# A selective-scan kernel on one NeuronCore: two groups of transposes, the first sum of each output group, and eight more C tokens change their places

## The chip, the cores and the metric

The kernel runs on one core of a Trainium2 chip. The metric is device time in microseconds (us) of one launch. Before the change it is 18172.63 us, the median of 3 runs (18170.29 to 18190.06).

The engines of the core are named as the profile names them: PE (TensorE, matmuls; its weight loads are PEld), DVE (VectorE), ACT (ScalarE), POOL (GpSimd) and SP (SyncE, which issues the DMAs). Each engine runs its own queue of instructions strictly in the order in which the program issued them, and waits at an instruction whose inputs or buffers are not ready.

## What is computed

Layer 0 is a convolution block (1x1 expand, 3x3 depthwise, squeeze and excite, 1x1 project) on a 32x96x56x56 image. Layer 1, which the change touches, applies two selective-scan blocks to the image's 3136 positions as a sequence, and then a fused 1x1 convolution with batch norm. Cut to what matters:

```python
xs, z = jnp.split(layernorm(seq) @ in_w, 2, axis=-1)
xc = silu(causal_conv4(xs))
dt, Bm, Cm = split(xc @ xproj_w)                 # 6 + 16 + 16 columns
delta = softplus(dt @ dt_w + dt_b)               # 192 channels
dA  = jnp.exp(delta[..., None] * A)              # 192 channels x 16 states
dBx = delta[..., None] * Bm[:, :, None, :] * xc[..., None]
h   = scan(h[t] = dA[t] * h[t-1] + dBx[t])       # along the 3136 tokens
y   = einsum('blds,bls->bld', h, Cm) + Dp * xc
seq = seq + (y * silu(z)) @ out_w
```

## The kernel before, in words

Layer 1 works in units. A unit is one chunk of 784 tokens (a quarter of an image) in one of the two scan blocks; there are 128 chunks, so 256 units. A unit has 192 x 16 = 3072 recurrences, which are 24 scans of 128 partitions x 784 tokens (`scan`, L1052, on DVE). The program is written by hand as one loop over steps, and a step is one scan. Scan t of a unit belongs to channel group k = t // 8 (three groups of 64 channels), to state quartet j = (t % 8) // 2, and to half p = t % 2.

A scan needs two inputs. `da` = exp(A delta) is made on ACT (`decay`, L1004). The other, delta x B, comes in two ways:

- For j = 1, 2, 3 POOL multiplies u = delta x by a broadcast B for a pair of scans, four steps ahead (`inject`, L1041).
- For j = 0, that is for scans 0, 1, 8, 9, 16 and 17, PE makes it in PSUM: `fill` (L1018) multiplies a transposed piece of u, the tile `ut`, by a diagonal arrangement of B. One fill is issued in the step before its scan. Its PSUM buffer is one of two that it shares with `da`, so it waits until the scan two before its own has ended. The tiles `ut` of a unit, one for each group k, are made by `turn_u` (L848: four PE transposes into one PSUM bank of a ring of two) and copied out by `keep_u` (L854 and L855, on ACT).

What follows a scan: its pair of results is multiplied by C, the first LP tokens of each half by DVE (`product`, L1060, from a copy of C that ACT puts into PSUM, `bring`, L1029), the rest by POOL (`rest`, L1068). PE sums the product over the states into the group's tile y (`reduce`, L1099, four matmuls a pair, LAG = 4 steps after the pair's second scan). Before a group's first sum, ACT puts Dp x into that tile (`seed`, L1086); since there is one y tile, this waits until DVE has multiplied the former group's finished y by z (`gated`, L1110, LAG + 1 steps behind).

Beside the scans, the same loop prepares later units and finishes the unit before: each helper has a due time in steps in the lists of `prepare` and `finish`. Due time 48 of a unit is its own scan 0. Within a step the fraction says where it is put: under 0.05 at the step's head, before `seed` and `decay`; 0.05 to 0.08 after `fill` and before `reduce`; from 0.08 on at the step's end. Before the change the transposes of the second group are due at 53.6 (end of step 5) and their copies at 54.2, those of the third group at 54.3 (end of step 6) and 55.01 (head of step 7); fills for the scans 8 and 9 are issued in the steps 7 and 8, those for 16 and 17 in 15 and 16.

Of the kernel before, what the change touches and what calls it, by code (L numbers as in the profile page):

```python
# [24 lines left out]
NL, NS, DIN, RANK, KC = 2, 16, 192, 6, 4  # L25
LC = 784
HB = LC // 2
LP = 416
NQ = L // LC
RB = HB // W  # L30
DG = 8
# [29 lines left out]
def conv_mamba_kernel(ctx, tc, a, out):  # L61
# [43 lines left out]
    with ExitStack() as ph:  # L105
# [119 lines left out]
        for i in range(NHB):  # L225
            t = hp3.tile([128, H + 2, W + 2], F32, name=f"hpad{i}", tag=f"hpad{i}")
# [303 lines left out]
    with ExitStack() as ph:  # L530
# [14 lines left out]
        def bank(name):  # L545
            return pp.tile([128, 512], F32, name=name, tag="p")

        def wt(shape, tag, bufs, n):
            return work.tile(shape, F32, name=f"{tag}_{n}", tag=tag, bufs=bufs)
# [135 lines left out]
        def prepare(n):  # L685
# [92 lines left out]
            def keep(tag, bufs, ps, k):  # L778
                if k == 0:
                    d[tag] = wt([128, NB, HB], tag, bufs, n)  # L780
                if tag == "dl":
                    s.activation(d[tag][:, k, :], d[ps, k][:, :HB], AF.Identity, bias=dp[:, i, k, 0:1])
                else:
                    s.copy(d[tag][:, k, :], d[ps, k][:, :HB])  # L784
# [22 lines left out]
            def project_dt(k):  # L807
                ps = d["dtp", k] = bank(f"dt_{n}_{k}")
                for r in both:
                    pe.matmul(ps[r, :HB], wd[r, i, k, :], d["bcs"][r, :], start=True, stop=True)  # L810
# [34 lines left out]
            def turn_u(k):  # L845
                ps = d["utp", k] = bank(f"ut_{n}_{k}")
                for b in range(4):
                    pe.transpose(ps[: TSZ[b], b * 128 : b * 128 + 128], d["us"][:, k, TOFF[b] : TOFF[b] + TSZ[b]], eye)  # L848

            def keep_u(k):  # L850
                ut = d["ut", k] = wt([TB, 4, 2, 64], "ut", 3, f"{n}_{k}")
                ps = d["utp", k].rearrange("p (b h m) -> p b h m", b=4, h=2)
                z = TSZ[-1]
                s.copy(ut[:, 0], ps[:TB, 0])  # L854
                s.copy(ut[:z, 1:], ps[:z, 1:])  # L855
# [11 lines left out]
            steps = [(-20.5, load)]  # L867
# [14 lines left out]
            steps += [(17.6, project_bc), (18.2, store_bc), (18.6, turn_b), (19.2, diagonal)]  # L882
            for k in range(NB):
                steps += [((20.6, 21.5, 21.6)[k], lambda k=k: project_dt(k)), ((21.2, 22.1, 22.2)[k], lambda k=k: keep("dl", 1, "dtp", k))]
                steps += [((43.5, 53.6, 54.3)[k], lambda k=k: turn_u(k)), ((44.1, 54.2, 55.01)[k], lambda k=k: keep_u(k))]
            for m in range(6):
                steps += [(26.9 + m, lambda m=m: scatter(*divmod(m, 3)))]
            steps += [(32.1, lambda: spread("delta", d["dl"], slice(0, NB)))]
# [54 lines left out]
        LAG = 4  # L943

        def place(t):
            k, r = divmod(t, 2 * SG)
            return k, r // 2, r % 2
# [38 lines left out]
        def by_pe(at):  # L986

            return place(at % NT)[1] == PEJ

        def lend(at):  # L990

            if by_pe(at) and at % 2 == 0:
                to = wt([128, 2, LC], "bx", 3, at)
                for p in range(2):
                    das[at + p] = to[:, p, :]

        def decay(at):

            n, t = divmod(at, NT)
            i, d = units[n][1], data[n]  # L1000
            k, j, p = place(t)
            if not by_pe(at):
                das[at] = dpool.tile([128, 2 * 512], F32, name=f"da_{at}", tag="da")[:, :LC]
            s.activation(das[at], d["delta", k][:, p, :], AF.Exp, scale=acol[:, j, i, 2 * k + p : 2 * k + p + 1])  # L1004
# [18 lines left out]
        def bring(at):  # L1023

            n, t = divmod(at, NT)
            k, j, p = place(t)
            if p == 1:
                cps[at] = cpool.tile([128, LP], F32, name=f"cp_{at}", tag="cp")
                s.copy(cps[at], data[n]["C", j][:, :LP])  # L1029

        def beside(x):

            return x.unsqueeze(1).to_broadcast([128, 2, x.shape[-1]])

        def inject(at):

            n, t = divmod(at, NT)
            k, j, p = place(t)
            if p == 0 and j != PEJ:
                bx = wt([128, 2, LC], "bx", 3, at)  # L1040
                g.tensor_mul(bx, data[n]["u", k], beside(data[n]["B", j]))  # L1041
                for p in range(2):
                    bxs[at + p] = bx[:, p, :]

        def scan(at):

            n, t = divmod(at, NT)
            (c, i), d = units[n], data[n]
            k, j, p = place(t)
            if p == 0:  # L1050
                hhs[at] = wt([128, 2, LC], "hh", 3, at)
            v.tensor_tensor_scan(  # L1052
                hhs[at - p][:, p, :], das.pop(at), bxs.pop(at), state[i][:, t : t + 1] if c % NQ else 0.0,
                ALU.mult, ALU.add,
            )

        def product(at):

            if place(at % NT)[2] == 1:
                v.tensor_mul(hcs[at - 1][:, :, :LP], hhs[at - 1][:, :, :LP], beside(cps.pop(at)))  # L1060

        def rest(at):

            n, t = divmod(at, NT)
            k, j, p = place(t)
            if p == 1:
                hcs[at - 1] = wt([128, 2, LC], "hc", 3, at)
                g.tensor_mul(hcs[at - 1][:, :, LP:], hhs[at - 1][:, :, LP:], beside(data[n]["C", j][:, LP:]))  # L1068

# [9 lines left out]
        def seed(at):  # L1079

            n, t = divmod(at, NT)
            k, j, p = place(t)
            if j == 0 and p == 1:
                i, d = units[n][1], data[n]
                yps[k] = ypool.tile([128, 512], F32, name=f"y_{n}_{k}", tag="y")
                s.activation(yps[k][:, :HB], d["xc"][:, k, :], AF.Copy, scale=dp[:, i, k, 1:2])  # L1086

        def reduce(at):

            n, t = divmod(at, NT)  # L1090
            i, d = units[n][1], data[n]
            k, j, p = place(t)
            if p == 0:
                return
            hc = hcs.pop(at - 1)
            for h in range(2):
                for p in range(2):
                    r0 = h * 64 + p * DB
                    pe.matmul(  # L1099
                        yps[k][r0 : r0 + DB, :HB], rel, hc[:, p, h * HB : h * HB + HB],  # L1100
                        start=False, stop=j == SG - 1, skip_group_check=True,
                    )
# [9 lines left out]
        total = len(units) * NT  # L1112
        todo, early = {}, {}
        for n in range(len(units)):
            steps, bursts = prepare(n)
# [9 lines left out]
        def ahead(at):  # L1125

            return (2, 1) if at % NT == 0 else (3, 2)
# [5 lines left out]
        with tc.manual_schedule():  # L1133
            for at in range(min(todo), max(todo) + 1):
                for m in (2, 3):
                    if 0 <= at + m < total and by_pe(at + m) and (at + m) % 2 == 0 and ahead(at + m)[0] == m:
                        lend(at + m)
                if 0 <= at + 4 < total:
                    inject(at + 4)
                for u, step in todo.get(at, ()):  # L1140
                    if u < 0.05:
                        step()
                if 0 <= at - LAG < total:
                    seed(at - LAG)
                if 0 <= at + 1 < total and not by_pe(at + 1):
                    decay(at + 1)
                for x in range(at, at + 5):
                    pair = x // 2 * 2
                    if 0 <= x < total and by_pe(x) and pair - ahead(pair)[x - pair] == at:
                        decay(x)  # L1150
                if 0 <= at < total:
                    bring(at)
                for step in early.get(at, ()):
                    step()
                if 0 <= at < total:
                    scan(at)
                if 0 <= at - LAG - 1 < total:
                    gated(at - LAG - 1)
                if 0 <= at - 1 < total:
                    product(at - 1)  # L1160
                if 0 <= at - 2 < total:
                    save(at - 2)
                if 0 <= at < total:
                    rest(at)
                if 0 <= at + 1 < total and by_pe(at + 1):
                    fill(at + 1)
                for u, step in todo.get(at, ()):
                    if 0.05 <= u < 0.08:
                        step()
                if 0 <= at - LAG < total:  # L1170
                    reduce(at - LAG)
                for u, step in todo.get(at, ()):
                    if u >= 0.08:
                        step()
                for t, tag in BEFORE[at % NT]:
                    fetch(at + t, (tag,))
# [79 lines left out]
```

## Time and profile before

The profiled execution took 18204.1 us; its span, first to last instruction, is 18202.3 us, and all times below are from its start.

| | |
|---|---|
| median of 3 runs | 18172.63 us |
| profiled execution / its span | 18204.1 / 18202.3 us |
| first scan starts, last scan starts | 3055.5 us, 17901.6 us |
| mean distance from one unit's scan 0 to the next one's (units 20 to 236) | 58.03 us |
| DVE / POOL busy per 1000 us, at 10000 to 11000 us | 944.43 / 949.15 us |
| ACT / PE busy in the same stretch | 846.78 / 866.13 us |
| mean granted TensorE clock | 0.912 |
| one scan / one product / one rest / one inject | 1.84 / 1.00 / 1.76 / 3.54 us |

A row of the timeline gives start, duration, engine, line, operation, output<-inputs, sizes and count, and in brackets how long the engine was idle before it and what ended that idle time. `x64` at a fill is its 32 matmuls, each recorded twice[...]; `x8` at a sum y is four matmuls. A row of the stretches gives, for each engine, the busy us and the number of instructions, and then PEclk, the share of the full TensorE clock that was granted.

### The profile page before, as it was taken

The numbers are of one execution on the slowest core, as the hardware profiler recorded it, in microseconds if no ns is written. First come the engines' busy times: TensorE is split into PE (matmuls) and PEld (weight loads), VectorE is DVE, ScalarE is ACT, GpSimd is POOL, SyncE is SP. The second block draws the span as 40 slices with busy tenths as digits, with TensorE's granted clock in tenths as the row PEclk, the third lists the DMA queues.
The fourth block names the chain that finished last, engine by engine and source line by source line (L and its number), as shares of the span: only waits on it lengthen the run. The fifth ranks groups of instructions, "written<-read, shape, count | busy, mean of one in ns | idle before, by whom it ended". The sixth has DMA issues, their size and how long they took to land.

```text
span 18202.3 us, 515600 instructions
## 1 busy us (share of the span) xinstructions
PE 15733.6 (86%) x212542; PEld 8423.4 (46%) x212542; DVE 16751.8 (92%) x12755; ACT 14204.1 (78%) x26476; POOL 14151.6 (78%) x6254
## 2 busy tenths in 40 slices
PE   9999998888888888888888888888888888888882
PEld 4444444444444444444444444444444444444441
DVE  9999996999999999999999999999999999999993
ACT  5555555888888888888888888888888888888884
POOL 0000002999999999999999999999999999999993
PEclk9999998999999999999999999999999999999996
DMA  1111113777777777777777777777777777777768
GB/s 35 29 29 29 29 29 88 182 183 183 182 185 186 184 183 183 183 183 186 184 183 182 183 182 186 184 184 183 183 183 184 186 183 182 184 182 182 186 182 220
DMA packets 1723533, 2893.14 MB, mean 159 GB/s; under 512 B 712886, under 2 KB 950670, under 8 KB 1714790
## 3 DMA queue, kind: packets, MB, share of 16 engines
q1 hardware_dynamic: 1712534, 2821.54, 59.6%
q0 software_dynamic: 6656, 38.54, 1.0%
q8 instruction: 1668, 27.33, 0.6%
q14 instruction: 691, 5.66, 0.1%
q10 hardware_dynamic: 1984, 0.07, 0.0%
HBM read 2402.42 MB, written 455.82 MB: 157 GB/s over the span
## 4 chain that ended last, share of the span: by engine, by line
PE 22%; ACT 16%; issue 12%; DMA 11%; DVE 9%; SPq 7%; POOL 5%; ACTq 0%; POOLq 0%; DVEq 0%
PE bp L1018 9%; DVE hh L1052 5%; ACT da L1004 5%; ACT bx L1004 4%; SPq L982 4%; DVE hc L1060 3%; DMA bdiag<-bt 3%; DMA deltab<-deltad 3%; PE y L1099 3%; SPq L969 3%; POOL hc L1068 2%; POOL bx L1041 2%; PE bc L798 2%; PE o L909 2%; DMA C<-bcd 2%
## 5 line engine op out<-in xcount | busy, mean ns | idle before, releaser
L1041 POOL TENSOR_TENSOR bx<-ub,B 128x1568 f32<-128x1568 f32 x2304 | 8160.7, 3542 | 16.2 <-DMA B<-bcd 16.2
L1052 DVE TENSOR_TENSOR_SCAN hh<-da,state,bx 128x784 f32<-128x784 f32 x3456 | 6257.5, 1835 | 53.1 <-ACT da L1004 50.2
L1068 POOL TENSOR_TENSOR hc<-hh,C 128x736 f32<-128x736 f32 x3072 | 5407.9, 1760 | 747.9 <-DVE hh L1052 476.0
L1004 ACT ACTIVATE da<-deltab,acol 128x784 f32<-128x784 f32 x4608 | 4253.4, 923 | 1192.4 <-DVE hh L1052 1184.8
L1099 PE MATMUL y<-hc,rel 128*32 128x392 f32 x24576 | 2888.8, 544 | 551.0 <-ACT y L1086 547.4
L1018 PEld LDWEIGHTS bp<-diag,ut 91*32 91x32 f32 (+1 forms) x98304 | 2873.9, 131 | 931.9 <-DVE hh L1052 544.1
L1018 PE MATMUL bp<-diag,ut 91*32 91x91 f32 (+1 forms) x98304 | 3192.1, 293 | 116.6 <-DVE hh L1052 100.7
L1060 DVE TENSOR_TENSOR hc<-hh,cp 128x832 f32<-128x832 f32 x3072 | 3065.6, 998 | 0.1
L1052 DVE TENSOR_TENSOR_SCAN hh<-bx,state,bp 128x784 f32<-128x784 f32 x1152 | 2116.7, 1837 | 491.3 <-PE bp L1018 488.6
masks.py:197 POOL MEMSET eye<- 128x128 f32 x2 | 0.4, 204 | 2923.3 <-ACT x L427 2923.0
L773 PE MATMUL xs<-xn,wx 97*64 97x392 f32 x12288 | 2250.3, 508 | 0.5 <-ACT xc L784 0.4
L1052 DVE TENSOR_TENSOR_SCAN hh<-da,bx 128x784 f32<-128x784 f32 x1152 | 2017.9, 1774 | 29.6 <-ACT da L1004 28.1
L340 DVE SCALAR_TENSOR_TENSOR h<-hpad,hp,h 128x1568 f32<-128x1568 f32 x1024 | 1895.3, 1851 | 33.2
L1029 ACT COPY cp<-C 128x416 f32<-128x416 f32 x3072 | 1576.4, 513 | 95.6 <-DVE hc L1060 93.3
L1004 ACT ACTIVATE bx<-deltab,acol 128x784 f32<-128x784 f32 x1536 | 1467.8, 956 | 0.0
L773 PEld LDWEIGHTS xs<-xn,wx 97*64 97x64 f32 x12288 | 816.5, 137 | 1357.4 <-issue 1264.4
L1099 PEld LDWEIGHTS y<-hc,rel 128*32 128x32 f32 x24576 | 623.9, 118 | 1523.9 <-ACT y L1086 1044.7
L307 PE MATMUL dw<-hpad,diag 32*32 32x392 f32 x36864 | 1124.8, 525 | 0.6 <-issue 0.4
L1052 DVE TENSOR_TENSOR_SCAN hh<-bx,bp 128x784 f32<-128x784 f32 x384 | 683.0, 1779 | 244.2 <-PE bp L1018 228.3
L245 PE MATMUL c<-x,w 96*128 96x392 f32 x2048 | 785.3, 526 | 118.2 <-ACT hpad L252 96.2
L848 PE MATMUL ut<-eye,us 128*91 128x128 f32 (+1 forms) x3072 | 582.3, 320 | 340.7 <-ACT xc L784 340.3
L307 PEld LDWEIGHTS dw<-hpad,diag 32*32 32x32 f32 x36864 | 680.8, 106 | 375.4 <-issue 132.0
(195 smaller groups left out, 20083.7 us busy)
## 6 DMA issues: line engine op xcount, KB each, us to landing
ub<-ud SPq DMA_DIRECT2D x3072, 196.0 KB
deltab<-deltad SPq DMA_DIRECT2D x3072, 196.0 KB
C<-bcd SPq DMA_DIRECT2D x4096, 98.0 KB
diag<-bdiag SPq DMA_DIRECT2D x1024, 294.8 KB
B<-bcd SPq DMA_DIRECT2D x3072, 98.0 KB
deltad<-dl SPq DMA_DIRECT2D x512, 294.0 KB
ud<-us SPq DMA_DIRECT2D x1536, 98.0 KB
x<-in_x_dram SPq DMA_DIRECT2D x32, 1176.0 KB
```

The costliest lines, as they stand in the source:

```text
L245: pe.matmul(ps[:p, k, :HB], w1[:, ct * 128 : ct * 128 + p], xs[b][:, c0 : c0 + HB], start=True, stop=True)
L307: pe.matmul(ps[r][to : to + 32, :HB], diag[src, n, t, :], hb[src, r0 : r0 + RB, dx : dx + W], start=t == 0, stop=t == 8, skip_group_check= ...
L340: v.scalar_tensor_tensor(acc, src, tap, acc, ALU.mult, ALU.add)
L773: pe.matmul(d["xs", k][h * 64 : h * 64 + 64, :HB], wx[:, i, o, k * 64 : k * 64 + 64], xn[:, o + h * HB : o + h * HB + HB], start=o == 0, s ...
L1004: s.activation(das[at], d["delta", k][:, p, :], AF.Exp, scale=acol[:, j, i, 2 * k + p : 2 * k + p + 1])
L1018: pe.matmul(ps[sg * DB : sg * DB + DB, o : o + z], d["ut", k][:z, b, h, p * DB : p * DB + DB], dg[:z, sg // 2, h, x : x + z, sg % 2], star ...
L1029: s.copy(cps[at], data[n]["C", j][:, :LP])
L1041: g.tensor_mul(bx, data[n]["u", k], beside(data[n]["B", j]))
L1052: v.tensor_tensor_scan(hhs[at - p][:, p, :], das.pop(at), bxs.pop(at), state[i][:, t : t + 1] if c % NQ else 0.0, ALU.mult, ALU.add,)
L1060: v.tensor_mul(hcs[at - 1][:, :, :LP], hhs[at - 1][:, :, :LP], beside(cps.pop(at)))
L1068: g.tensor_mul(hcs[at - 1][:, :, LP:], hhs[at - 1][:, :, LP:], beside(data[n]["C", j][:, LP:]))
L1099: pe.matmul(yps[k][r0 : r0 + DB, :HB], rel, hc[:, p, h * HB : h * HB + HB], start=False, stop=j == SG - 1, skip_group_check=True,)
```

## The change

Four edits. The transposes of the second group (`turn_u(1)`) go from the end of step 5 to the end of step 0, and their copies to the head of step 1. Those of the third group go from the end of step 6 to step 8, behind the fill for scan 9, and their copies to the head of step 9. For each group, `seed` and the first sum of y (that of the PE-made pair, j = 0) are issued one step later; the other sums stay. And LP grows from 416 to 424 tokens, so that each product on DVE takes 16 more elements a partition, each rest on POOL 16 fewer, and each copy of C 8 more.

```diff
-LP = 416
+LP = 424
...
             for k in range(NB):
...
-                steps += [((43.5, 53.6, 54.3)[k], lambda k=k: turn_u(k)), ((44.1, 54.2, 55.01)[k], lambda k=k: keep_u(k))]
+                steps += [((43.5, 48.5, 56.06)[k], lambda k=k: turn_u(k)), ((44.1, 49.01, 57.01)[k], lambda k=k: keep_u(k))]
...
-                if 0 <= at - LAG < total:
-                    seed(at - LAG)
+                if 0 <= at - LAG - 1 < total:
+                    seed(at - LAG - 1)
...
-                if 0 <= at - LAG < total:
-                    reduce(at - LAG)
+                for t in (at - LAG - 1, at - LAG):
+                    if 0 <= t < total and by_pe(t) == (t == at - LAG - 1):
+                        reduce(t)
```

## The prediction

> **What bounds the kernel now.** First the page's busy line, then the waits of DVE.
>
> ```profile
> PE 15733.6 (86%) x212542; PEld 8423.4 (46%) x212542; DVE 16751.8 (92%) x12755; ACT 14204.1 (78%) x26476; POOL 14151.6 (78%) x6254
> ...
> L1052 DVE TENSOR_TENSOR_SCAN hh<-bx,state,bp 128x784 f32<-128x784 f32 x1152 | 2116.7, 1837 | 491.3 <-PE bp L1018 488.6
> ```
> ```profile
> DVE hh L1052 <- PE bp L1018: 716.9, 647, 2.3
> ...
> DVE hh L1052 <- ACT da L1004: 78.3, 249, 1.0
> ```
>
> DVE is the chain: in layer 1 it works 94.4% of the time, and nearly all its idle time is before scans fed by a fill. Averaged over units 20 to 236, a unit of 58.03 us has DVE idle 1.95 us before scan 8, 0.59 and 0.30 before scans 16 and 17 (all for fills), 0.11 and 0.20 before scans 18 and 20 (for `da`): 3.15 us. POOL is next: 94.9% busy, 55.1 us a unit, and its idle 2 us are mostly before the rest of pair 20/21, waiting for DVE.
>
> Why is the fill for scan 8 late? PE in a unit whose scan 0 starts at 10073.98:
>
> ```profile
> 10085.76 0.86 PE L1099 MATMUL y<-hc,rel 128*32 128x392 f32 x8 [1.59 <-ACT y L1086]
> 10086.55 1.54 PE L773 MATMUL xs<-xn,wx 97*64 97x392 f32 x8
> 10088.37 0.65 PE L848 MATMUL ut<-eye,us 128*120 128x128 f32 x4 [0.28 <-ACT xc L784]
> 10090.43 0.65 PE L848 MATMUL ut<-eye,us 128*120 128x128 f32 x4 [1.41 <-ACT xc L784]
> 10091.01 2.85 PE L1018 MATMUL bp<-diag,ut 120*32 120x120 f32 x64
> 10093.64 1.20 PE L1099 MATMUL y<-hc,rel 128*32 128x392 f32 x8
> ```
> ```profile
> 10087.60:10091.00 3.40, 1.71 (x12) 0.87 (x8) 3.40 (x4) 3.32 (x8) 3.01 (x2) 0.99 0.87 203
> 10091.00:10094.40 3.40, 3.40 (x73) 2.90 (x76) 1.58 (x2) 3.25 (x5) 3.40 (x2) 0.50 0.70 188
> 10108.10:10111.50 3.40, 3.07 (x44) 3.04 (x48) 3.40 (x3) 2.93 (x5) 3.40 (x3) 0.50 0.91 222
> ```
>
> Three waits in a row: the first sum waits for the seed, which waits for DVE's gating; each transpose then waits for a PSUM bank that ACT must empty. So the fill starts at 17.0 us of the unit, though its buffer was free at 15.5 (end of scan 6). And it runs at half clock: the stretch before had PE half idle, the stretch of the fill was granted 0.50. A fill takes 1.66 us at full clock and 2.85 at half.
>
> Over the whole trace the clock records change in steps of 3.413 us. Of the full-clock windows of that length in layer 1, those with under 50% of matmul work (transposes L848 and the one-column variances L712 not counted) were followed by half clock 403 times in 405, those over 55% never in 1886. So I can tell where the change will halve the clock. Half clock ends after a window over about 62%. One more thing: 58.03 us is 17.00 such windows, and the unit keeps its phase to them all through the layer; the pace is locked to the clock gate.
>
> **The change part by part** (positions in us from the unit's scan 0).
>
> *Second group's transposes to step 0.* PE: 0.65 us more behind the fill for scan 1 (ends 1.80), less at 14.4. ACT must now do the copies (0.63) before `da` of scan 2. Queue there: `da` 2, the C copy, `da` 3; DVE's scan 2 waits for the first. Chain: fill ends 1.80, transposes 2.4, copies 3.1, `da` 4.0; scan 2 is due at 4.41. Covered by 0.4, so nothing; without that cover up to 1.3 (were this fill at half clock).
>
> *First sums a step later.* ACT loses a wait of 1.26 for the gating; its own chain then gives: `da` 6 at 10.7, `da` 8, C copy, xc copy 13.0 to 13.5, seed to 13.9. PE: the third projection runs unbroken to 12.4, waits 1.5 for the seed, sums to 14.8, and stands free when scan 6 ends. Fill 8 starts at 15.6 instead of 17.0: 15.6 + 1.67 = 17.3 at full clock, 18.45 at half, against 18.15 when DVE is ready. In the third group the sum (0.86, or 1.53 at half) falls between the variances and fill 16, and so onto the path.
>
> *Clock around fill 8.* PE will be idle 1.5 us before the sum and 0.8 after. Sliding a 3.413 us window over this, the 50 to 55% limit is undershot for ends from 15.0 to 16.5, 45% of all phases. Here the Trainium skill speaks (TensorE: Matmul & The Clock Gate, section "HAM oscillation — how this bites in real kernels"): only gaps over about 3.4 us between bursts bring the clock down. By that rule no gap here counts, fill 8 would be at full speed always and all PE waits of 2.85 would go: some 660 us off. The rows above show 0.50 after gaps of at most 1.6, so I take the trace. Wait before scan 8: 0 or 0.3.
>
> *Third group's transposes behind fill 9.* PE: 0.65 after fill 9 (ends 19.9 full, 20.9 half). ACT: the copies stand ahead of `da` 10, and behind them the C copy and `da` 11. At full clock ACT leaves the softplus and its table loads at 21.0, copies 21.7, `da` 22.65: scan 10 waits 0.1. At half: transposes 21.6, copies 22.25, `da` 23.2, against 22.7: 0.5. This wait is new. The output projection wants the same bank ring: its second half waits for the copies, under 0.5 on PE, in cover. POOL's first u product of the next unit (single buffer) now waits for these transposes: 21.6 at latest, POOL arrives near 24.5, cover 2.9. No DMA is in any moved step, and SP's and POOL's orders are the same.
>
> Sum for the second group: 1.95 before; after it 0.1 in 55% of phases, 0.6 in 45%: 0.35. Gain 1.6.
>
> *Third group.* Before, fills 16 and 17 cost 0.89. PE's gap from the centring (L702) to fill 16 gets longer without a sum in its middle: 30.4 to 34.0 is all idle or one-column work, so one half window always falls in 32 to 39, as before. DVE arrives 1.5 us earlier (scan 16 due near 36.9), PE only 0.9. If the half window starts before 33.2, it isn't ended by enough work: fill 16 runs 35.5 to 38.4, wait 1.5 to 1.6. If later, 0.6 to 1.1. Nearest row: waits of 0.76 and 1.46 in single units before. I take 1.25: 0.35 lost. Bounds 0.45 and 2.0. ACT's `da` 18 keeps within 0.1 (its chain is about 1.1 earlier too).
>
> *Last group's sum behind both dt projections.* PE: fill 0 of the next unit starts 0.3 later; cover 0.45. 0.05 for the cases at half clock; bounds 0 and 0.7.
>
> *424 tokens.* DVE: 998 ns for 832 elements, 16 more: 19 ns at most, 12 a unit: 0.23 lost, on the path (below it only if the row has a large fixed part, then 0.1). POOL 38 ns x 12 = 0.46 less: hidden, it waits for DVE. ACT 0.1, hidden.
>
> Sum: 1.6 - 0.35 - 0.05 - 0.23 = 0.97 a unit. The phase no longer locks at 17 windows: it wanders, slowly where a unit is nearest 58.03, so slow phases count more; I take 0.88, a pace of 57.15. Over 254 units 224 us: from the profiled 18204 to 17980. The median of runs is 31 below the profiled execution, so 17950.
>
> **The rivals.**
>
> *The lock holds (13%).* Slow phases as worked out are 57.6 to 57.75; 0.3 us more of misjudged waits, and units again reach 58.03 in some phase. Then the phase stops there, and the time stays 18173 whatever was saved. For: the lock before, though single units range from 57.6 to 58.4. Against: two thirds of the phases should be well under.
>
> *The half clock settles on the third group (slower, 10%).* The sum moved in front of fill 16 runs at half clock, fill 16 ends near 39, and y and fill 17 follow at half too. Before, all fills cost 2.85 a unit; with the 0.23 for the products, the change loses once scans 8 to 10, 16 and 17 together wait over 2.6. Price with 0.6 + 1.85 + 0.9 = 3.35: 58.03 - 2.85 + 0.23 + 3.35 = 58.76, 185 us more: 18360. Against: that needs two half windows in every unit, and fill 17 normally lies beyond them.
>
> *Full clock through both groups (12%).* If the remaining gaps stay over the limit, DVE's own work of 55.1 plus 0.3 for `da` remains, and POOL's 54.6 is under it: 55.6 to 56.3, 440 to 620 us off: 17555 to 17735.
>
> *The change as summed (65%).* Bounds of the third group's and the wrap's cost give 56.5 to 57.8: 17785 to 18115.
>
> **Numbers.** Predicted 17950. The range 17760 to 18175 takes in the likeliest case, its nearer half of the full-clock case and the lock; the slower case and the far end of the gain stay out. About 0.2% (36 us) is what a measurement here tells from no change. Faster: 65 + 12 = 77%; same 13%; slower 10%.
>
> **What would show it.** The waits of DVE for bp should fall from 717 to 350 to 450 us in total; those for `da` rise from 78 to 100 to 200, with scan 10 new among them. Fill 8 should start right at the end of scan 6, in about half the units at half clock. ACT's wait for the gating (351 us) should vanish. DVE's products should take near 1017 ns, POOL's rests near 1722. I am wrong if the pace is still 58.03 (lock), if scan 2 waits for `da` (cover of the early transposes gone), or if waits at scans 16 and 17 have doubled.

## The result, and the profile after

The changed kernel takes 18228.22 us, the median of 12 runs (18205.65 to 18249.94), against 18180.30 us for the kernel before (12 runs, 18165.60 to 18201.86). The ratio is 1.0026, with a 95% interval of 1.0019 to 1.0034: slower, by a little over the 0.2% that was called measurable. The forecast was 17950, and the range ended at 18175.

The profiled execution has a span of 18222.0 us, 20 more than before, and its mean granted clock is 0.905 instead of 0.912. The first fence holds lines of the page: the busy time of each engine, then rests, products and the scans that are fed by a fill.

```profile
PE 15695.8 (86%) x212542; PEld 8470.5 (46%) x212542; DVE 16828.1 (92%) x12755; ACT 14197.5 (78%) x26476; POOL 14050.8 (77%) x6254
...
L1068 POOL TENSOR_TENSOR hc<-hh,C 128x720 f32<-128x720 f32 x3072 | 5319.2, 1732 | 896.4 <-DVE hh L1052 490.1
...
L1060 DVE TENSOR_TENSOR hc<-hh,cp 128x848 f32<-128x848 f32 x3072 | 3121.4, 1016 | 0.1
L1052 DVE TENSOR_TENSOR_SCAN hh<-bx,state,bp 128x784 f32<-128x784 f32 x1152 | 2120.5, 1841 | 450.2 <-PE bp L1018 432.1
```

The products take 1016 ns (1017 was forecast), the rests 1732 (1722). The idle time before scans fed by a fill was to halve; on this row it went from 491 to 450. The waits of DVE, in us, times and longest:

```profile
DVE hh L1052 <- PE bp L1018: 604.1, 620, 15.4
DVE hh L1052 <- ACT da L1004: 131.4, 408, 1.7
...
DVE hh L1052 <- POOL bx L1041: 42.8, 43, 1.5
```

Waits for fills fell from 717 to 604 (350 to 450 was forecast); 15.4 of the 604 is one wait before the very first scan, which the list of the kernel before puts down to ACT. Those for `da` rose from 78 to 131 (100 to 200 was forecast). POOL is named at 43 more waits, and at none before; in units 20 to 236 they stand before scans 0, 10 and 16, and are counted there below. ACT's wait for the gating, 351 us before, is gone from the list.

Sorted by scan, the mean wait before each scan over units 20 to 236, in us a unit, is this:

| scan | 0 | 8 | 9 | 10 | 16 | 17 | 18 | 20 | all |
|---|---|---|---|---|---|---|---|---|---|
| before | 0 | 1.95 | 0.01 | 0 | 0.59 | 0.30 | 0.11 | 0.20 | 3.16 |
| after | 0.18 | 0.26 | 0.42 | 0.18 | 1.61 | 0.01 | 0 | 0.35 | 3.03 |

So 1.69 us went from scan 8 and 0.40 from scans 17 and 18, and 1.94 came back at scans 0, 9, 10, 16 and 20. DVE is also busy 0.31 us longer a unit (55.10 against 54.79), 0.22 of it in the products. The pace went from 58.03 to 58.22.

Where it came back is seen in the unit whose scan 0 starts at 9552.06. PE around the fills for scans 8 and 9 (rows: start, duration, what, and in brackets PE's idle time before):

```profile
9562.10 2.15 PE L773 MATMUL xs<-xn,wx 97*64 97x392 f32 x12
9566.02 1.20 PE L1099 MATMUL y<-hc,rel 128*32 128x392 f32 x8 [1.77 <-ACT y L1086]
9567.70 2.85 PE L1018 MATMUL bp<-diag,ut 120*32 120x120 f32 x64 [0.48 <-DVE hh L1052]
9570.33 1.53 PE L1099 MATMUL y<-hc,rel 128*32 128x392 f32 x8
9571.63 2.35 PE L1018 MATMUL bp<-diag,ut 120*32 120x120 f32 x64
```

The order is as planned. The fill for scan 8 starts at 15.6 us of the unit, when scan 6 ends; its own stall is gone. But it takes 2.85 us, the sum behind it 1.53, and the fill for scan 9 2.35 instead of 1.66. The next view, PE alone in three windows of the clock, shows why (busy us and count, then PEclk; the last two figures are of the DMA):

```profile
9563.00:9566.41 3.41, 1.64 (x16) 1.00 0.60 139
9566.41:9569.83 3.42, 2.94 (x60) 0.50 0.96 225
9569.83:9573.24 3.41, 3.41 (x68) 0.50 0.49 135
```

PE is busy for 1.64 of 3.41 us (48%), and the clock is halved. Then it is busy for 2.94 of 3.42 (86%), and stays at half for another window. That second window is what the forecast did not have. DVE waits 0.35 before scan 8 and 0.59 before scan 9 in this unit.

The third group, in the unit whose scan 0 starts at 12059.71, first PE's rows and then DVE's:

```profile
12090.30 0.73 PE L712 MATMUL var<-mean,sx 96*112 96x1 f32 x6
12092.79 1.65 PE L712 MATMUL var<-mean,sx 96*112 96x1 f32 x8 [1.76 <-ACT sx L707]
12094.37 1.53 PE L1099 MATMUL y<-hc,rel 128*32 128x392 f32 x8
12095.68 2.85 PE L1018 MATMUL bp<-diag,ut 120*32 120x120 f32 x64
```
```profile
12094.81 1.84 DVE L1052 TENSOR_TENSOR_SCAN hh<-da,state,bx 128x784 f32<-128x784 f32 x1
12098.66 1.85 DVE L1052 TENSOR_TENSOR_SCAN hh<-bx,state,bp 128x784 f32<-128x784 f32 x1 [2.00 <-PE bp L1018]
```

And the windows of the clock there, with the busy us and count of PE, PEld, DVE, ACT and POOL before PEclk:

```profile
12088.87:12092.28 3.41, 2.16 (x11) 1.08 (x10) 3.41 (x5) 3.18 (x7) 3.41 (x3) 1.00 0.08 19
12092.28:12095.69 3.41, 2.90 (x19) 1.97 (x22) 3.41 (x3) 3.39 (x7) 3.41 (x4) 0.50 0.84 210
```

The clock was halved at 12092.28 for two windows; of the 2.16 us of PE before that, 0.73 are one-column variances. Variances, sum and fill then stand one behind another at half speed, 5.7 us in all, and scan 16 waits 2.00.

### The profile page after: what moved, and what is told of

Its sections match the earlier page's. It is cut to its first block, busy times and chain, and to the rows that moved or that the text cites. A ratio compares the mean times of both kernels' runs of the same rounds, so it can differ in the third digit from the quotient of the medians.

```text
span 18222.0 us, 516622 instructions
## 1 busy us (share of the span) xinstructions
PE 15695.8 (86%) x212542; PEld 8470.5 (46%) x212542; DVE 16828.1 (92%) x12755; ACT 14197.5 (78%) x26476; POOL 14050.8 (77%) x6254
## 4 chain that ended last, share of the span: by engine, by line
PE 29%; DVE 18%; issue 17%; ACT 12%; POOL 3%; DMA 3%; SPq 2%; ACTq 0%; DVEq 0%; POOLq 0%
DVE hh L1052 11%; PE bp L1018 9%; DVE hc L1060 6%; PE y L1099 5%; ACT da L1004 3%; PE z L789 3%; PE bc L798 3%; PE o L909 3%; ACT bx L1004 2%; PE var L712 1%; ACT sx_t L751 1%; ACT cp L1029 1%; PE o L905 1%; POOL bx L1041 1%; POOL hc L1068 1%
## 5 line engine op out<-in xcount | busy, mean ns | idle before, releaser
L1068 POOL TENSOR_TENSOR hc<-hh,C 128x720 f32<-128x720 f32 x3072 | 5319.2, 1732 | 896.4 <-DVE hh L1052 490.1
L1018 PEld LDWEIGHTS bp<-diag,ut 91*32 91x32 f32 (+1 forms) x98304 | 2963.9, 133 | 1322.6 <-DVE hh L1052 748.1
L1099 PE MATMUL y<-hc,rel 128*32 128x392 f32 x24576 | 3017.0, 566 | 471.5 <-ACT y L1086 468.8
L1060 DVE TENSOR_TENSOR hc<-hh,cp 128x848 f32<-128x848 f32 x3072 | 3121.4, 1016 | 0.1
L773 PE MATMUL xs<-xn,wx 97*64 97x392 f32 x12288 | 2140.3, 497 | 0.0
L1029 ACT COPY cp<-C 128x424 f32<-128x424 f32 x3072 | 1592.2, 518 | 140.2 <-DVE hc L1060 136.6
L712 PE MATMUL var<-mean,sx 96*112 96x1 f32 x3584 | 514.3, 262 | 462.0 <-ACT sx L707 462.0
L798 PE MATMUL bc<-xc,wbc 64*64 64x392 f32 x3072 | 582.7, 510 | 338.2 <-DVE rs L734 330.8
```

The costliest lines, as they stand in the source:

```text
L773: pe.matmul(d["xs", k][h * 64 : h * 64 + 64, :HB], wx[:, i, o, k * 64 : k * 64 + 64], xn[:, o + h * HB : o + h * HB + HB], start=o == 0, s ...
L798: pe.matmul(ps[r, :HB], wbc[r, i, k], d["xc"][r, k, :], start=k == 0, stop=k == NB - 1)
L1018: pe.matmul(ps[sg * DB : sg * DB + DB, o : o + z], d["ut", k][:z, b, h, p * DB : p * DB + DB], dg[:z, sg // 2, h, x : x + z, sg % 2], star ...
L1099: pe.matmul(yps[k][r0 : r0 + DB, :HB], rel, hc[:, p, h * HB : h * HB + HB], start=False, stop=j == SG - 1, skip_group_check=True,)
```

## The experiments

The first theory behind the failure was the clock: the late sums thin out PE's work just before the fills, and half clock is granted at the fills of both groups. Its rival was the order: the sums stand in front of the fills, and cost what they last, whatever the clock. A third theory was the lock: the pace is held near 17 windows of 3.413 us (the steps in which the clock records change), 58.03 us.

All results in one table: ratio to the kernel before with its 95% interval, and in us a unit the pace, the time at half clock and the waits before the scans named.

| kernel | ratio | pace | half clock | 8 to 10 | 16, 17 | 18, 20 | 0 |
|---|---|---|---|---|---|---|---|
| before | | 58.03 | 9.9 | 1.96 | 0.89 | 0.31 | 0 |
| after | 1.0026 [1.0019, 1.0034] | 58.22 | 11.3 | 0.86 | 1.62 | 0.35 | 0.18 |
| after, PE's gaps filled (e1) | 0.9832 [0.9819, 0.9845] | 56.71 | 5.0 | 0.01 | 0.20 | 0.97 | 0.22 |
| before, PE's gaps filled (e2) | 0.9866 [0.9852, 0.9879] | 57.00 | 5.3 | 1.19 | 0.11 | 0.58 | 0 |
| after, 416 tokens (e3) | 1.0000 [0.9992, 1.0008] | 58.03 | 11.8 | 0.56 | 2.00 | 0.30 | 0.24 |
| transposes only (e4) | 0.9741 [0.9728, 0.9754] | 56.16 | 5.2 | 0.04 | 0.92 | 0.29 | 0.02 |
| sums only (e5) | 1.0060 [1.0048, 1.0073] | 58.44 | 11.4 | 1.88 | 0.94 | 0.45 | 0.17 |
| after, middle sum back (e6) | 0.9844 [0.9831, 0.9858] | 56.84 | 8.3 | 0.41 | 0.67 | 0.29 | 0.28 |
| after, first gap filled (e7) | 0.9961 [0.9948, 0.9973] | 57.71 | 9.0 | 0.01 | 1.97 | 0.28 | 0.45 |
| e4 with 424 tokens (e9) | 0.9775 [0.9761, 0.9788] | 56.39 | 5.8 | 0.06 | 0.81 | 0.36 | 0 |
| e4, gaps filled (e10) | 0.9648 [0.9634, 0.9661] | 55.49 | 2.0 | 0.04 | 0.14 | 0.38 | 0.03 |
| e4, first group's sum late (e11) | 0.9762 [0.9748, 0.9775] | 56.30 | 6.7 | 0.18 | 0.79 | 0.31 | 0.01 |
| e4, second group's sum late (e12) | 0.9865 [0.9851, 0.9878] | 57.07 | 7.0 | 0.10 | 1.81 | 0.32 | 0.02 |
| e4, last group's sum late (e13) | 0.9758 [0.9745, 0.9771] | 56.35 | 6.2 | 0.06 | 0.63 | 0.40 | 0.26 |
| e4, first two sums late (e14) | 0.9959 [0.9947, 0.9972] | 57.76 | 10.4 | 0.63 | 1.77 | 0.32 | 0.10 |
| e4, last two sums late (e15) | 0.9964 [0.9951, 0.9976] | 57.71 | 9.2 | 0.03 | 2.04 | 0.30 | 0.52 |
| e10 with all sums late (e16) | 0.9818 [0.9805, 0.9832] | 56.62 | 6.2 | 0.57 | 0.51 | 0.34 | 0.16 |
| e10, second sum late (e17) | 0.9677 [0.9664, 0.9690] | 55.70 | 2.4 | 0.03 | 0.45 | 0.33 | 0.03 |

The second group's sum is the one that stands just before the fill for scan 16, the first group's the one before the fill for scan 8, and the last group's the one before the fill for the next unit's scan 0.

**Fill PE's gaps with work that changes nothing (e1, e2).** A few matmuls are issued again with the same inputs into the same PSUM tile; the real ones begin that tile anew, so the output is computed in full. Put in: the first tap of the third projection twice more, and the second half's centring twice more.

```diff
+                for _ in range(2 if k == 2 and taps[0] == 0 else 0):
+                    for h in range(2):
+                        pe.matmul(
+                            d["xs", k][h * 64 : h * 64 + 64, :HB], wx[:, i, 0, k * 64 : k * 64 + 64],
+                            xn[:, h * HB : h * HB + HB], start=True, stop=True,
+                        )
...
-                pe.matmul(ps[:C, :HB], cen, seqs[c, i][:, cols(h)], start=True, stop=True)
+                for _ in range(3 if h == 1 else 1):
+                    pe.matmul(ps[:C, :HB], cen, seqs[c, i][:, cols(h)], start=True, stop=True)
```

> The changed kernel with PE kept busy in its two long idle stretches: the first tap of the third projection is computed three times instead of once (four matmuls, 1.4 us more, in the 1.7 us before the first sum), and the second half of the centring three times (two matmuls, 1.55 us more, in the 1.85 us before the second half of the variances). Results are the same. Theory clock (the change opened idle stretches that halve PE's clock, and the waits moved to scans 9 and 16): fills 8, 9 and 16 run at full clock in 1.67 us, waits for fills fall from 604 us to under 200, the pace goes from 58.2 to 55.9 to 56.6 us a unit, ratio to the kernel before 0.970 to 0.982. Theory order (the waits come from the order of instructions on ACT and PE, the clock only goes along): 3 us a unit of extra PE work cannot help; ratio 1.00 to 1.02.

> The kernel before with the same extra matmuls. Its transposes still wait for their PSUM bank in the stretch ahead of fill 8. Theory clock: fill 8 stays late and at half clock (wait 1.9), only fill 16 goes to full clock; waits for fills fall from 2.8 to 2.0 us a unit, ratio 0.985 to 0.995, or 1.000 if the pace stays locked at 17 windows of 3.413 us. Theory order: 1.00 to 1.02.

More work on PE, and both kernels are faster: the changed one went from 1.0026 to 0.9832. The order of the sums and fills is the same, so the order theory can't explain it. DVE's waits of the changed kernel with its gaps filled (seven lines further down the code):

```profile
DVE hh L1059 <- ACT da L1011: 245.3, 392, 1.7
...
DVE hh L1059 <- PE bp L1025: 96.6, 142, 13.5
```

The wait for fills is 97 us instead of 604. That for `da` is up to 245, and 122 of 216 units have half clock elsewhere, at 41 to 57 us of the unit, where the changed kernel had it in 84: filling a gap moves the thin place on. With gaps filled in both, the change is worth 0.3% (0.9832 against 0.9866), not the 1.2% of the forecast.

**Leave out the tokens (e3).** `LP = 416` in the changed kernel; all else as changed.

> The changed kernel with 416 tokens. DVE does 0.23 us a unit less; with all else equal 58 us off the change: ratio 0.9995. If the pace is held near 17 windows of the clock gate by its waits, the saved work turns into waiting and the ratio stays 1.002 to 1.004.

The ratio is 1.0000, and the pace 16.9998 windows of 3.4133 us: with its DVE work back at 832 elements, the kernel stands on the old lock. It waits as long as before, in other places.

**Each half of the change alone (e4, e5).** Of the change only the transposes' due times (e4, shown), or only the sums (e5, the other edits of the change's diff), both with 416 tokens:

```diff
-                steps += [((43.5, 53.6, 54.3)[k], lambda k=k: turn_u(k)), ((44.1, 54.2, 55.01)[k], lambda k=k: keep_u(k))]
+                steps += [((43.5, 48.5, 56.06)[k], lambda k=k: turn_u(k)), ((44.1, 49.01, 57.01)[k], lambda k=k: keep_u(k))]
```

> Of the change only the two moved groups of transposes; sums of y at their old steps, 416 tokens. Theory clock: fill 8 starts at 15.6 as in the change, PE's idle stretch ahead of it is split in two by the first sum, and the stretch ahead of fill 16 is as before (wait 0.9): about 57 us a unit, ratio 0.980 to 0.995, or 1.000 if the pace locks at 58.03. Theory order: scan 10 waits for the copies as in the change, ratio 0.995 to 1.005.

> Of the change only the first sums of y a step later; transposes at their old steps, 416 tokens. Theory clock: the transposes still stand in front of fill 8 and idle time ahead of fill 16 is longer: waits before scan 8 stay at 1.5 to 2, those before scan 16 rise to 1.5; ratio 1.005 to 1.015. Theory order: about the same, 1.000 to 1.010.

The transposes alone bring 2.6%, more than twice the whole forecast; the sums alone cost 0.6%. DVE's waits with the transposes only:

```profile
DVE hh L1052 <- PE bp L1018: 255.6, 349, 15.4
...
DVE hh L1052 <- ACT da L1004: 67.3, 234, 1.0
```

And PE before the fill for scan 8 there, in a unit whose scan 0 starts at 9057.29:

```profile
9069.07 0.87 PE L1099 MATMUL y<-hc,rel 128*32 128x392 f32 x8 [0.88 <-ACT y L1086]
9069.87 1.54 PE L773 MATMUL xs<-xn,wx 97*64 97x392 f32 x8
9072.88 1.67 PE L1018 MATMUL bp<-diag,ut 120*32 120x120 f32 x64 [1.47 <-DVE hh L1052]
```

This fill, too, starts at 15.6 us of its unit and waits only for scan 6. The sum need not move for that: once the transposes are gone, its old place is early enough. And it does good there. PE's idle time before the fill, 0.88 + 1.47 us, is about that of the changed kernel, 1.77 + 0.48, but sum and projection lie between the two parts. The 3.41 us that end where the fill starts hold 1.94 us of PE work (57%) here:

```profile
9069.47:9072.88 3.41, 1.94 (x17) 0.48 (x9) 3.41 (x3) 3.41 (x6) 3.04 (x2) 1.00 0.91 141
```

In the unit of the changed kernel above, the same stretch before its fill (9564.29 to 9567.70) holds 1.20 us (35%). The means over 216 units are 1.97 and 1.04. Half clock comes before the fill for scan 8 in 12 of 216 units here, in 177 with the change, and in 104 with only this sum late (e11).

**The tokens on the transposes (e9).** The kernel with the transposes only, and `LP = 424`.

> The two moved groups of transposes together with 424 tokens; sums of y at their old steps. If a product's extra 19 ns on DVE lie on the path, 12 of them make 0.23 us a unit: about 58 us over the transposes alone (ratio 0.974 becomes 0.977). If POOL were the limit, 0.46 us a unit less: 0.968. If the phase to the clock gate decides, anything from 0.968 to 0.985.

They cost 0.0034, 0.23 us a unit: the price that was forecast for DVE, in full.

**The transposes with the gaps filled (e10).** As in e1 for the centring; in place of the projection's tap, the four matmuls of L744 that make the first tokens' centred transposes (`turn(0)`) are issued twice.

```diff
-                for k in TURNS[m]:
+                for k in tuple(TURNS[m]) * (2 if m == 0 else 1):
```

> The moved transposes alone, with PE kept busy where it still idles: the second half of the centring three times, and the first four matmuls of the transposed sequence (L744) twice. Results are the same. Theory clock: what is left before scans 16 and 17 (0.58 and 0.34) goes, the half clock around the B and C projection as well; pace 55.2 to 55.7, ratio 0.958 to 0.968. Theory order: the extra 2.5 us of PE work delay fill 16; ratio 0.975 to 0.99.

The best kernel of the study: 17542.64 us. DVE's waits (one line further down the code):

```profile
DVE hh L1053 <- ACT da L1005: 87.0, 228, 1.6
DVE hh L1053 <- PE bp L1019: 67.0, 117, 14.1
```

**One late sum at a time (e11, e12, e13).** On the kernel with the transposes only; with g = 0, 1 or 2:

```diff
-                if 0 <= at - LAG < total:
-                    seed(at - LAG)
+                for t in (at - LAG - 1, at - LAG):
+                    if 0 <= t < total and (t % NT // 8 == g) == (t == at - LAG - 1):
+                        seed(t)
...
-                if 0 <= at - LAG < total:
-                    reduce(at - LAG)
+                for t in (at - LAG - 1, at - LAG):
+                    if 0 <= t < total and (by_pe(t) and t % NT // 8 == g) == (t == at - LAG - 1):
+                        reduce(t)
```

> Transposes moved, 416 tokens, and only the first sum of the first group a step later. Theory clock: PE's idle time ahead of fill 8 (0.9 and 1.5, parted by the sum) becomes 1.5 in one piece and 0.75; fills 8 and 9 are at half clock in about half the units, scans 8 to 10 wait 0.5 to 0.9 together; pace 56.6 to 57.1, ratio 0.980 to 0.990. Theory order: the sum is ready before fill 8 is due in either place; ratio 0.974 as without it.

> Transposes moved, 416 tokens, and only the first sum of the second group a step later, so that it stands between the variances and fill 16. Both theories: fill 16 starts later by the sum; wait before scan 16 from 0.58 to 1.2 to 1.6, before 17 from 0.34 to 0. Theory clock adds that the idle stretch is now 1.8 us with nothing in it, so nearly every fill 16 is at half clock: pace 56.6 to 57.2, ratio 0.980 to 0.992. If the loss of the change came from the first group alone: 0.974 to 0.978.

> Transposes moved, 416 tokens, and only the first sum of the third group a step later, behind both dt projections. By the working of the prediction fill 0 of the next unit comes 0.3 us later inside a cover of 0.45: ratio 0.974 to 0.978. If this edit carries what the parts measured so far leave open of the loss (tokens 0.0034, first group's sum 0.0021, second's 0.0124, of 0.0285): 0.980 to 0.988, with waits at scan 0 and half clock between 50 and 56 us of the unit.

They cost 0.0021, 0.0124 and 0.0017. The dear one is the sum in front of the fill for scan 16: that scan waits 1.78 us instead of 0.58. The other two are hardly over what two such ratios can tell apart.

**Put only that sum back (e6).** The changed kernel, with `seed` and first sum of the second group at their old step.

```diff
-                if 0 <= at - LAG - 1 < total:
-                    seed(at - LAG - 1)
+                for t in (at - LAG - 1, at - LAG):
+                    if 0 <= t < total and (t % NT // 8 == 1) == (t == at - LAG):
+                        seed(t)
...
-                    if 0 <= t < total and by_pe(t) == (t == at - LAG - 1):
+                    if 0 <= t < total and (by_pe(t) and t % NT // 8 != 1) == (t == at - LAG - 1):
```

> The changed kernel with the second group's first sum back at its old step; all else as in the change. If the parts add, 0.0124 less than the change: ratio 0.990. If the sum of the second group is what keeps the unit slow in all phases and the other parts cost only what they cost alone, 0.980 to 0.984. If the first group's waits (scans 8 to 10: 0.87 us a unit) are their own matter and stay: 0.988 to 0.996.

0.9844: this single part undone turns the loss of 0.3% into a gain of 1.6%.

**Fill only the first gap (e7).** The changed kernel with the repeated projection taps of e1, without the repeated centring.

> The changed kernel with PE kept busy only ahead of the first sum (first tap of the third projection three times, 1.4 us). Theory clock: fills 8 and 9 run at full clock, the 0.87 us of waits at scans 8 to 10 go, those before scan 16 stay at 1.3 to 1.8; pace 57.2 to 57.6, ratio 0.984 to 0.994. Theory order: no gain, 1.00 to 1.01.

The waits at scans 8 to 10 fall from 0.86 to 0.01, but the pace only by 0.51: scan 16 now waits 1.95 instead of 1.61. A unit that is early at scan 8 has to wait at scan 16 for the same fill at half clock.

**Two late sums at a time (e14, e15).** The edit of e11 to e13, with `in (0, 1)` or `in (1, 2)` in place of `== g`.

> The kernel before with both transpose edits and with the first sums of the first two groups one step later; 416 tokens, the last group's sum as before. Alone, on the transposes, the first group's sum cost 0.14 us a unit and the second group's 0.91 (paces 56.30 and 57.07 against 56.16). If the parts add up: pace 57.2, ratio to before 0.989. If units near 17 windows of the clock gate are pulled to 58.03 and held there: pace 57.5 to 58.0, ratio 0.993 to 1.000, and many units within 0.2 us of 58.03.

> The same with the first sums of the second and the last group late, and the first group's as before. If the parts add up (0.91 and 0.19 us a unit): pace 57.25, ratio 0.988. If the pull of the 17 windows is at work as soon as a second cost stands beside the second group's: pace over 57.5, ratio over 0.993.

One by one the parts would give 0.0145 and 0.0141; the pairs cost 0.0218 and 0.0223, and all three (e3) 0.0259 instead of 0.0162. The parts don't add up. That the rest is a hold near 17 windows fits the paces, but isn't shown by them: in e14 106 of 216 units lie within 0.3 us of 58.03, in e15 74, in e4 6.

**The sums with the gaps filled (e16, e17).** e10 with the late sums of all groups (416 tokens), and with that of the second group. What the first expectation calls the first group's transposes of x are the matmuls of L744.

> The transposes and all three late sums with 416 tokens, as in the run that saved the tokens (ratio 1.0000), and besides PE's idle stretches partly filled with repeats of matmuls that give the same result again (the centring three times, the first group's transposes of x twice), as in the run of 0.9648. If the late sums cost what they cost by their place in PE's order, they cost 0.026 here too: ratio 0.990. If they cost it by the half clock that they let in, most of it goes: half clock under 5 us a unit, ratio 0.970 to 0.978.

> The same repeats and the transposes, with only the second group's first sum late. Place in PE's order: 0.9 us a unit as without the repeats, ratio 0.977. Half clock: 0.2 us a unit or less, ratio 0.965 to 0.969, wait before scan 16 under 0.5 us (1.78 without the repeats).

The second group's sum costs 0.0029 with the gaps filled and 0.0124 without: about three quarters of its price is half clock. PE in a unit of e17 without half clock, with variances, sum and fill in the order of the changed kernel:

```profile
10182.65 0.95 PE L713 MATMUL var<-mean,sx 96*112 96x1 f32 x8 [0.70 <-ACT sx L708]
10183.53 0.87 PE L1100 MATMUL y<-hc,rel 128*32 128x392 f32 x8
10184.21 1.66 PE L1019 MATMUL bp<-diag,ut 120*32 120x120 f32 x64
```

They take 3.2 us instead of 5.7, and scan 16 doesn't wait. All three sums together still cost 0.0170 with these repeats (0.0259 without), above the 0.970 to 0.978 that was expected of the clock alone. The gap before the fill for scan 8 isn't filled in e16, and the waits at scans 8 to 10 are back at 0.57 with 6.2 us of half clock. The units of e16 tell how much of this is order. The 50 of 216 without any half clock wait 0.01 us at scans 8 to 10 and nothing at 16 and 17, and take 55.04 us each; the 166 with it wait 0.74 and 0.67, and take 57.10. So, as far as units that came that way can show it, all three sums may stand late and cost nothing at these scans while the clock is full; the order then matters by how often the clock is halved.

## Why the prediction was wrong

**What held.** The places. The seed ends at 13.9 us of the unit and the first sum at 14.7 (forecast 13.9 and 14.8), the fill for scan 8 starts at 15.6, and scan 2 does not wait for the early transposes' copies. The tokens cost 0.22 us a unit in the products (0.23 was forecast). The third group's transposes behind the fill for scan 9 do little harm: in e4 the wait before scan 10 is 0.03.

**What failed: "Clock around fill 8", the share and the length.** The geometry of the gap was right: half clock sets in at 14.3 to 16.0 us, half of all phases (45% was taken). But units do not visit the phases evenly, and 177 of 216 had it. In 113 of these it lasted two windows, so that the fill for scan 9 ran at half clock as well: it ended at 22.1 us, where the working had 20.9, and scan 9 waited 0.79. The sum priced that in no case. With none, one and two windows the waits at scans 8 to 10 are 0.01, 0.43 and 1.42 us; the sum had 0.1 and 0.6 (0.3 and 0.5, the waits that it names for half clock, add to 0.8).

The limit for halving held in the main. With L848 and L712 left out as in the forecast, and all windows of layer 1 counted, 429 of 434 full-clock windows with under 50% of work were followed by half clock after the change (406 of 408 before), and 70 of 2955 over 55% (none of 2969 before). The limit for recovery, "over about 62%", did not hold. Of the half-clock windows with 65 to 95% of work, 120 of 128 recovered in the kernel before, and 122 of 281 after the change. It was read from a kernel that kept its phase, and so from the same few mixes of work over and over. So the step that gave 0.35 for scans 8 to 10 measured 0.86.

**"Third group".** 1.25 was taken with bounds of 0.45 and 2.0; it measured 1.62. 103 units had two half windows there, with 2.17 before scan 16, and 113 had one, with 1.10. The mechanism was named (a sum at half clock in front of the fill), its bad case was priced at 1.5 to 1.6, and it was worse than that. E6 shows that this part alone decides the sign.

**"Last group's sum".** 0.18 before scan 0, not 0.05.

Together: 0.51 + 0.37 + 0.13 = 1.01 us a unit of misjudged waits, where the forecast gain was 0.97.

**The gain was put to the wrong edit.** The steps credited the start of the fill at 15.6 to the late sum. e4 shows the transposes alone give it, and that the sum at its old place keeps the clock up. The part that was priced at nothing and at 0.1 to 0.5 us of new waits is the whole gain. How it divides between the second and the third group's transposes was not tried.

**The lock.** The rival "the lock holds" set its own condition: 0.3 us more of misjudged waits. That was met three times over, and what followed can be read from the paces by half windows near the fill for scan 8: 57.13 us with none, 58.28 with one, 58.56 with two. The first is shorter than 17 windows and the others are longer, so a unit without half clock moves the phase one way and a unit with it moves it back, and the phase stays about the place where half clock begins. In e4 the means of both kinds (56.11 and 56.99) lie below 58.03, and the phase runs through. In e3 the pace is 17.000 windows. The changed kernel isn't fixed in the same way: its mean is 17.055, and 10 units with half clock for three windows at 41 to 57 us take 60.35 each. Over units 20 to 236 it falls behind 17 windows a unit by 12.0 windows in all, 6.8 of them in these ten units; 12 x 3.413 us over 216 units are 0.19 us, the whole rise of the pace. The kernel before and e3 fall behind by 0.0, and the sums alone (e5) by 26.0, with 26 units of that kind. Read by the phase, then, the changed kernel still stood on the lock, where what is saved turns into waiting, and now and then lost a whole window besides. That these paces attract the phase fits the runs in which they were taken apart; a run with the phase forced was not made.

**The slower rival** was priced at 18360 by half windows settled on the third group in every unit, and was to decide once scans 8 to 10, 16 and 17 wait over 2.6 us. They wait 2.48; the 0.18 at scan 0 and the 0.31 of DVE work (0.23 was taken) do the rest. It was close to the truth, and 10% was too little: with the third group at 2.0 and the last group's sum at 0.7, the working's own bounds, the sum gives a pace of 58.47, while the bounds of the likeliest case were given as 56.5 to 57.8. The range also took in less than was said: the full-clock case was priced at 17555 to 17735, all of it below 17760.

**The clock rule.** The Trainium skill's 3.4 us gap (TensorE: Matmul & The Clock Gate, section "HAM oscillation — how this bites in real kernels") was rightly set aside: no gap of PE in its rows around the fill for scan 8 is over 1.77 us, and the clock is halved. Nearer is the same page's section "A second HAM failure mode: psum-queue depth-cycling", by which frequent short idle times between groups of matmuls make the clock swing too. The runs agree, and add a price: in e10 less idle time at the same order took 0.9% off (0.9648 against 0.9741).

## What to carry to other kernels

Where a matmul engine is neither the bound nor fully busy, its idle time has a place as well as a length: work that is moved towards a late, critical matmul can leave the window before it thin, and the matmul then runs at half clock (2.85 us here instead of 1.66). Move the smallest part first and look at the granted clock of the windows around the critical work; here two of the four edits were worth 2.6%, and the other two gave all of it back. And a rule for the clock that is fitted on a kernel locked to one phase may hold only for the mixes of work that this phase shows; here the limit for recovery did not carry over.

## What was unexpected of the hardware

- Useless matmuls pay: with 1536 more of them over the whole run (3072 records) than e4, e10 is 165 us faster, and its half clock falls from 5.2 to 2.0 us a unit.
- Recovery from half clock can fail in a window in which PE is 86% busy (2.94 of 3.42 us above). Another window, around the fill for scan 8 in the unit that starts at 12059.71, has 3.27 of 3.41 and recovers:

```profile
12075.21:12078.62 3.41, 3.27 (x68) 2.79 (x72) 3.06 (x4) 2.87 (x5) 3.41 (x2) 0.50 0.95 229
```

- What the clock counts is not settled. Transposes and one-column matmuls were left out of the count because that separated well in the kernel before; the exceptions (70 over 55%) are not explained. For recovery another count fits both kernels better: with the transposes of L848 counted and only L712 left out, a limit of 90% misjudges 7 of 750 half-clock windows before and 27 of 844 after, where 62% of the first count misjudges 11 and 170. It was fitted afterwards, and in e5 it is no better (72 of 860 against 67).
